# Group norm and layer norm ahead of a selective scan: GpSimd adds the two channel tiles of batches 1 to 3 before TensorE takes means and variances

## The chip, the cores and the metric

The kernel runs on one core of a Trainium2 chip. The core has five engines with a queue each: TensorE (PE in the profile, with its weight loads as PEld), VectorE (DVE), ScalarE (ACT), GpSimd (POOL) and SyncE (SP, which here only issues DMAs). They run side by side and wait for each other by semaphores. The metric is the device time of one execution in microseconds (us), as a median of several runs; lower is better. All data are fp32 unless a line says bf16.

## The reference, cut to what matters

The network has two layers on an input `x` of 4 batches x 256 channels x 1024 tokens. Layer 0 is a block with a group norm, a layer norm, four Mamba scans, attention and convolutions; layer 1 is attention and a mixture of experts. The change touches the first two norms of layer 0 alone:

```
def _gn(v, G=32, eps=1e-5):
    B_, C_, H_, W_ = v.shape
    g = v.reshape(B_, G, C_ // G, H_, W_)
    m = jnp.mean(g, axis=(2, 3, 4), keepdims=True)
    s = jnp.var(g, axis=(2, 3, 4), keepdims=True)
    return ((g - m) / jnp.sqrt(s + eps)).reshape(v.shape)

def layernorm(x, w, b, eps=1e-05):
    mu = x.mean(-1, keepdims=True)
    var = ((x - mu) ** 2).mean(-1, keepdims=True)
    return (x - mu) * jax.lax.rsqrt(var + eps) * w + b

x = x + _L0_conv_ref(_gn(x), ...)      # and inside it:
    xs = x.reshape(B, Cc, N).transpose(0, 2, 1)
    xn = layernorm(xs, norm_w, norm_b)          # over the 256 channels of each token
    xc = xn.reshape(B, N, NB, DM).transpose(2, 0, 1, 3)
    xm = mamba_v(xc, ...) + skip_scale * xc     # four independent selective scans
```

The layer norm needs, for each token, the mean and the variance over all 256 channels.

## The kernel before, in words

**Layout.** A batch is held as two channel tiles (`CT` = 2) of 128 partitions x 1024 tokens, `x[0]` and `x[1]`, and handled in halves of 512 tokens (`HALVES`). A sum over channels is a sum over partitions and over the two tiles, so it is done on TensorE.

**The norms of one batch, `normalise(b)` (L559 on).** Group norm: DVE sums of each tile (L568), a small matmul that adds them up by group (L569), squares with a running sum on ACT (L574), a second small matmul (L577), a copy (L580) and the inverse root by `small_root` (L548 to L557, a Newton iteration of twelve small DVE operations), then scale and shift in place (L586). Layer norm: for each half, TensorE multiplies a 128x128 matrix `avg` with 1/256 in each place by `x[0]` and then `x[1]`, accumulated in one PSUM bank, which leaves the mean of each token in all partitions (L592 to L595). DVE subtracts it from both tiles (L598). ACT writes the squares of both tiles to `sq` (L603), which is the place in `XM[b]` that the normalised batch will fill at last. The variance (L610 to L616) is taken the other way round: each block of 128 tokens of `sq` is the stationary operand and one column of `avg` the moving one, for both tiles, which leaves one column per block: 16 matmuls of one column. DVE copies them (L619) and runs `small_root` on 128x8. The result is put on the diagonal of `r` (L629: DVE for batch 0, POOL for the others), replicated to all partitions by a matmul with ones (L638), copied back to `r` by ACT (L652), and POOL multiplies both tiles by it (L654, 128x1024 each); ACT applies weight and bias (L656). For batch 0 a part of this is done by DVE and ACT straight from PSUM (L644, L648).

**The first front, `first_front` (L699 on).** For batch 0's first scan: a causal convolution as matmuls on 64 rows (L714, eight records for each half), SiLU (L717), two small projections (L720 and L750), a softplus (L722 to L731, in which DVE's L726 and L727 and POOL's L728 follow each other half by half), a DMA of `ds` (L732), a split of an fp32 tensor into three bf16 parts (L735 to L739), and the gathering of these parts into `U` by DMAs that SP and POOL issue (L744).

**The planner.** These two are not issued as written. Each operation is put in a plan with an engine, an estimated cost in ns, and what it reads and writes (`add(engine, cost, function, reads, writes, ...)`); `pre.run()` (L830) then sorts them by these estimates. Batch 0 and the first front are the plan's main line; `normalise(1)` to `normalise(3)` are added under `pre.beside(-1, -1, low=True)` (L821), which lets them fill gaps. So the order on every engine's queue follows the estimates. Results that stay in PSUM take one of a few banks (`pre.bank()`).

**Batch 3.** Its variances and the root are not part of the plan but of the list `behind`, (0, var) and (1, root): the first scan steps issue them, and later steps the diagonal (step 3), the replication (step 6) and the multiplication (from step 13).

**The scan loop (L832 on).** 256 steps in a written order; the scan is along the tokens, one step for each block of state rows. Step t: DVE multiplies the selected rows by B (L837), runs the scan over 1024 tokens (L840), POOL multiplies by C (L841); PE selects the rows of step t+2 (`select`, L778, from `U`), adds up the outputs of step t-2 (L789), SP fetches step t+4 (`fetch`, L766), ACT prepares step t+3 (`decay`, L771, an Exp of `dA` in place). Steps 0 and 1 are selected, and steps 0 to 2 decayed, by the plan. The next batch's front (L403 to L432) is mixed in by steps. `dBu`, which select fills, has two PSUM buffers, which the plan's banks share at first; in the trace the select of step 1 waits for scan 0.

After the loop come the rest of layer 0, layer 1's attention and the experts, which the change doesn't touch.

Of the kernel before, what the change touches and what calls it, by code (L numbers as in the profile page):

```python
# [13 lines left out]
ALU = mybir.AluOpType  # L14
# [6 lines left out]
P = 128  # L21
CT = C // P
# [136 lines left out]
class Plan:  # L159
# [32 lines left out]
    def add(self, engine, ns, emit, reads=(), writes=(), bank=None, take=False, give=False, pos=None, lag=0):  # L192
        reads, writes = list(reads), list(writes)
        banks = bank if isinstance(bank, list) else [] if bank is None else [bank]
        for bank in banks:
            (reads if give or engine != "PE" else writes).extend(bank.keys)
        deps = []
        for k in reads:
            if k in self.writer:
                deps.append(self.writer[k])  # L200
        for k in writes:
            deps.extend(self.readers.get(k, ()))
            if k in self.writer:
                deps.append(self.writer[k])
        op = dict(
            engine=engine, ns=ns, emit=emit, deps=deps, banks=banks, take=take, give=give, pos=pos, lag=lag,
            end=None, at=None, n=self.count,
        )
        self.count += 1
        for bank in banks:  # L210
            bank.ops.append(op)
        for k in reads:
            self.readers.setdefault(k, []).append(op)
        for k in writes:
            self.writer[k], self.readers[k] = op, []
        if self.group is None:
            self.main.setdefault(engine, []).append(op)
        else:
            self.group.append(op)
            self.side.setdefault(engine, []).append(op)  # L220
        return op
# [95 lines left out]
def body(tc, g, out):  # L317
    nc = tc.nc
    act, mm = nc.scalar.activation, nc.tensor.matmul
    ts, tt, stt = nc.vector.tensor_scalar, nc.vector.tensor_tensor, nc.vector.scalar_tensor_tensor  # L320
    HALVES = (slice(0, 512), slice(512, 1024))
# [4 lines left out]
    with pool("const", 1) as cp, pool("dram", 1, space=bass.MemoryType.DRAM) as drp, contextlib.ExitStack() as late:  # L326
# [7 lines left out]
        ident, grp, avg = cst[:, 0:P], cst[:, P : 2 * P], cst[:, 2 * P : 3 * P]  # L334
# [38 lines left out]
        with pool("mconst", 1) as mc, pool("front", 1) as fp, pool("dts", 2, space=bass.MemoryType.DRAM) as dsp, pool(  # L373
# [123 lines left out]
            with pool("scan", 6) as sp, pool("yps", 1, space=PSUM) as yps, pool("dps", 2, space=PSUM) as dps, pool("lnA", 1) as wp:  # L497
# [44 lines left out]
                def XS(b, ks=range(CT), hs=range(2)):  # L542
                    return [("xs", b, k, h) for k in ks for h in hs]

                def XN(b, ks=range(CT), hs=range(2)):
                    return [("xn", b, k, h) for k in ks for h in hs]
# [12 lines left out]
                def normalise(b):  # L559

                    x, r = xs[b], roots[b]

                    sq = dst = XM[b][:, :, XL : XL + N]
                    cols = slice(b * CT, (b + 1) * CT)
                    mine = [("gn", b)]
                    for k in range(CT):
                        j = b * CT + k
# [3 lines left out]
                    for k in range(CT):  # L571
                        j = b * CT + k
# [10 lines left out]
                    for k in range(CT):  # L583
                        j = b * CT + k
# [4 lines left out]
                    for h in range(2):  # L589
                        bank = pre.bank()  # L590

                        def mean(h=h, bank=bank):  # L592
                            for k in range(CT):
                                mm(bank.t, avg, x[k][:, HALVES[h]], start=k == 0, stop=k == CT - 1)
                        add("PE", 1720, mean, XS(b, hs=[h]), (), bank, take=True)  # L595
                        for k in range(CT):
                            add(
                                "DVE", 690, lambda k=k, h=h, bank=bank: tt(x[k][:, HALVES[h]], x[k][:, HALVES[h]], bank.t, ALU.subtract),  # L598
                                XS(b, [k], [h]), XS(b, [k], [h]), bank, give=k == CT - 1,
                            )  # L600
# [6 lines left out]
                    last = b == B - 1  # L607
                    bank = pre.bank()

                    def var():  # L610
                        for j in range(NT):
                            for k in range(CT):
                                mm(
                                    third[:, 520 + j : 521 + j] if last else bank.t[:, j : j + 1],
                                    sq[:, k, j * P : (j + 1) * P], avg[:, 0:1], start=k == 0, stop=k == CT - 1,
                                )  # L616

                    def root():
# [3 lines left out]
                    if last:  # L622
                        behind.extend([(0, var), (1, root)])
                        return
                    add("PE", 3500, var, XN(b), (), bank, take=True)
                    add("DVE", 2100, root, (), [("small", b)], bank, give=True)

                    def diagonal():
# [181 lines left out]
                with pre.beside(-1, -1):  # L810
                    weights()
                normalise(0)
                first_front()
                for t in range(4):
# [6 lines left out]
                with pre.beside(-1, -1, low=True):  # L821
                    for b in range(1, B):
                        normalise(b)
                    for i, step in fronts[1]:
                        if i < 0:
                            add("PE" if i < -1 else "ACT", 1720 if i < -1 else 1150, step, XN(0, [0]) + ["m_cu"], ["mm"])
# [4 lines left out]
                with tc.manual_schedule():  # L831
                    for t in range(NBLK + 9):  # L832
                        n, j = t // NJ, t % NJ
                        if t < NBLK:
# [4 lines left out]
                            hs = hss[t] = sp.tile([P, N], F32, tag="hs", name="hs")  # L839
# [35 lines left out]
        with pool("sets", 1) as wp, pool("work", 1) as kp, pool("ps2", 1, space=PSUM) as ps:  # L875
# [44 lines left out]
            add = plan.add  # L920
# [923 lines left out]
            for i in range(B * NT + 2):  # L1844
                b, unit = i // NT, (i - 2) // HT
# [25 lines left out]
        with pool("fin", 3) as fp, pool("rows", 1) as yp, pool("pfin", 4, space=PSUM) as pf:  # L1871
# [5 lines left out]
            for u in range(2 * B):  # L1877
                b, half = u // 2, u % 2
# [20 lines left out]
```

## Time and profile before

| | |
|---|---|
| runs | 3181.12, 3185.66, 3192.16 us (median 3185.66) |
| profiled execution | 3180.55 us, of which the profile's span is 3178.8 us |
| granted TensorE clock, mean of the span | 0.941 |
| busy over the span | PE 88%, DVE 64%, ACT 48%, POOL 39% |
| norms and first front | 0 to about 101 us |
| scan loop | about 101 to 1080 us |

How the profile is read: each instruction of one execution has a start and a duration, on its engine and with its line in the kernel. A row of a timeline has the start in us from the span's start, the duration, engine, line, operation, the output and input by the program's names, shape and type, and how many instructions were merged. Brackets say how long the engine sat idle before, and what released it. An f32 matmul shows as two records, so `x8` is four matmuls. PEclk is the clock that was granted to TensorE, 1.00 being full speed; it takes the values 0.5 and 1, and stretches show their mean. "q" after an engine's name is its instruction queue.

### The profile page before, as it was taken

The numbers are of one execution on the slowest core, as the hardware profiler recorded it, in microseconds if no ns is written. First come the engines' busy times: TensorE is split into PE (matmuls) and PEld (weight loads), VectorE is DVE, ScalarE is ACT, GpSimd is POOL, SyncE is SP. The second block draws the span as 40 slices with busy tenths as digits, with TensorE's granted clock in tenths as the row PEclk, the third lists the DMA queues.
The fourth block names the chain that finished last, engine by engine and source line by source line (L and its number), as shares of the span: only waits on it lengthen the run. The fifth ranks groups of instructions, "written<-read, shape, count | busy, mean of one in ns | idle before, by whom it ended". The sixth has DMA issues, their size and how long they took to land. (4 is left out here: it accounts for less than half of the span.)

```text
span 3178.8 us, 38805 instructions
## 1 busy us (share of the span) xinstructions
PE 2802.7 (88%) x15292; PEld 1592.1 (50%) x15292; DVE 2050.0 (64%) x2336; ACT 1533.2 (48%) x2102; POOL 1251.8 (39%) x790
## 2 busy tenths in 40 slices
PE   6788888888898689998899889988979998799996
PEld 3322222222222135555546455555536666699996
DVE  5799999999999656564866585486264545411112
ACT  3666566566655316455845764666343332211111
POOL 0687877777777500000100010001132334666662
PEclk7899999999989879999999989999989999899998
DMA  3576776676667400000000000000000002455445
GB/s 131 146 175 159 183 176 164 171 186 165 167 173 177 152 0 1 1 1 28 1 1 1 27 1 1 14 1 1 14 0 14 7 14 75 124 145 165 90 125 163
DMA packets 92874, 265.53 MB, mean 84 GB/s; under 512 B 18182, under 2 KB 36086, under 8 KB 89360
## 3 DMA queue, kind: packets, MB, share of 16 engines
q1 hardware_dynamic: 64000, 198.46, 23.6%
q0 software_dynamic: 26512, 60.35, 7.4%
q10 hardware_dynamic: 2176, 4.19, 0.3%
q8 instruction: 123, 2.02, 0.3%
q14 instruction: 63, 0.52, 0.1%
HBM read 291.70 MB, written 42.80 MB: 105 GB/s over the span
## 5 line engine op out<-in xcount | busy, mean ns | idle before, releaser
L841 POOL TENSOR_TENSOR hs<-hs,bc 128x1024 f32<-128x1024 f32 x256 | 603.2, 2357 | 246.4 <-DVE hs L840 236.1
L840 DVE TENSOR_TENSOR_SCAN hs<-dA,dBu 128x1024 f32<-128x1024 f32 x256 | 585.3, 2286 | 30.8 <-DVE dBu L837 1.9
L1106 DVE TENSOR_REDUCE nm<-s 128x1 f32<-128x1024 f32 x256 | 301.5, 1219 | 194.9 <-PE s L1101 193.9
L1111 ACT ACTIVATE pr<-s,nm 128x1024 f32<-128x1024 f32 x256 | 284.9, 1115 | 188.4 <-DVE nm L1106 185.7
L771 ACT ACTIVATE dA<-dA,aneg 128x1024 f32<-128x1024 f32 x256 | 289.1, 1145 | 164.7 <-DMA dA<-ds 155.1
L1125 PE MATMUL k<-const,pr 128*128 128x128 f32 x2048 | 296.4, 288 | 76.9 <-ACT pr L1111 51.1
L1125 PEld LDWEIGHTS k<-const,pr 128*128 128x128 f32 x2048 | 230.2, 145 | 186.1 <-ACT pr L1111 75.2
L837 DVE TENSOR_TENSOR dBu<-dBu,bc 128x1024 f32<-128x1024 f32 x256 | 309.9, 1211 | 18.3 <-PE dBu L778 18.1
L1175 POOL TENSOR_TENSOR b<-b 128x1024 f32<-128x1024 f32 (+1 forms) x15 | 30.3, 2019 | 684.6 <-ACT b L1171 665.3
L1101 PE MATMUL s<-b,b 32*128 32x512 f32 x1024 | 290.4, 654 | 5.1 <-ACT pr L1111 5.1
L778 PE MATMUL dBu<-U,pick 96*128 96x512 bf16 x512 | 161.9, 399 | 126.6 <-DVE hs L840 126.5
L1131 ACT COPY pT<-k 128x512 f32<-128x512 f32 x320 | 174.6, 592 | 171.0 <-PE k L1125 169.8
L789 PE MATMUL pY<-hs,const 128*128 128x512 f32 x512 | 243.1, 597 | 9.6 <-DVE u L481 9.6
L1774 PE MATMUL s<-pT,b 128*128 128x128 f32 x1920 | 236.0, 280 | 7.4 <-DMA b<-we,intse 6.2
L1774 PEld LDWEIGHTS s<-pT,b 128*128 128x128 f32 x1920 | 231.4, 196 | 13.2 <-issue 6.8
L778 PEld LDWEIGHTS <-pick 96*128 96x128 bf16 x512 | 34.6, 98 | 328.0 <-DVE hs L840 213.8
L1778 DVE TENSOR_TENSOR pT<-pT,s 128x512 f32<-128x512 f32 x72 | 49.3, 685 | 229.8 <-ACT pT L1777 229.6
L1131 DVE COPY pT<-k 128x512 f32<-128x512 f32 x192 | 131.4, 686 | 78.8 <-PE k L1125 74.7
L1145 PE MATMUL k<-pT,b 128*32 128x128 f32 x4096 | 150.0, 287 | 6.2 <-ACT pT L1131 4.0
L1101 PEld LDWEIGHTS s<-b,b 32*128 32x128 f32 x1024 | 104.3, 191 | 94.5 <-issue 76.5
L1145 PEld LDWEIGHTS k<-pT,b 128*32 128x32 f32 x4096 | 111.7, 114 | 69.9 <-issue 37.9
L789 PEld LDWEIGHTS pY<-hs,const 128*128 128x128 f32 x512 | 96.4, 191 | 98.1 <-issue 81.9
(445 smaller groups left out, 4647.6 us busy)
## 6 DMA issues: line engine op xcount, KB each, us to landing
dA<-ds SPq DMA_DIRECT2D x256, 512.0 KB, 4.7
dq<-parts SPq DMA_DIRECT2D x15, 768.0 KB, 4.2
U<-dq SPq DMA_DIRECT2D x45, 256.0 KB, 6.1
ds<-dt SPq DMA_DIRECT2D x16, 512.0 KB, 2.9
b<-x SPq DMA_DIRECT2D x4, 1024.0 KB, 7.1
acc<-pr SPq DMA_DIRECT2D x8, 512.0 KB, 7.6
xm<-x SPq DMA_DIRECT2D x4, 1024.0 KB, 5.0
tokens<-pr SPq DMA_DIRECT2D x8, 512.0 KB, 2.9
```

What stands on the lines that cost most here:

```text
L771: act(dAs[t], dAs[t], AF.Exp, scale=aneg[:, c : c + 1])
L789: mm(r["pY"][:, h], strip[:, P - DB - j * DB : 2 * P - DB - j * DB], hs[:, h], start=p == 0, stop=p == NJ - 1)
L837: tt(dBu, dBu, r["B"], ALU.mult)
L840: nc.vector.tensor_tensor_scan(hs, dAs.pop(t), dBu, 0.0, ALU.mult, ALU.add)
L841: nc.gpsimd.tensor_tensor(hs, hs, r["C"], ALU.mult)
L1101: mm(S[i][:, HALVES[h]], qT[rr, qt * P : (qt + 1) * P], kT[rr, HALVES[h]], start=True, stop=True)
L1106: "DVE", 1220, lambda i=i, u=u: nc.vector.tensor_reduce(nms[u], S[i], AX.X, ALU.max, negate=True),
L1111: "ACT", 1330, lambda i=i, u=u, hd=hd: act(prs[u % 4], S[i], AF.Exp, bias=nms[u], scale=1.0, accum_out=rss[b % 2][:, k, qt, hd : hd + 1]), ...
L1125: nc.tensor.transpose(bank.t[:, j * P : (j + 1) * P], prs[u][:, c0 : c0 + P], ident)
L1131: lambda dst=dst, bank=bank, on_act=on_act: (nc.scalar.copy if on_act else nc.vector.tensor_copy)(dst, bank.t),
L1145: mm(bank.t[i * HD : (i + 1) * HD, 0:P], v[:, 4 * jh + j, hd * HD : (hd + 1) * HD], pTs[m][jh][:, i, j * P : (j + 1) * P], start=j == 0, s ...
L1774: mm(p12[:, a, c], wbufs[w][:, o : o + P], xT[:, k], start=k == 0, stop=k == CT - 1)
```

## The change

For batches 1 to 3 POOL adds the two tiles of a half into `sq[:, 0]` before the mean, so that one matmul per half is left of two; and after ACT's squares POOL adds `sq[:, 1]` to `sq[:, 0]`, half by half, so that eight one-column matmuls are left of sixteen. `sq[:, 0]` is used twice, first for the sums and then for the squares. Batch 0 stays as it is. The estimates in the plan change with it: each addition 1180 on POOL, the mean 860 instead of 1720, the variance 1800 instead of 3500. For batch 3 the additions before the variance are part of the plan, and the variance itself stays in `behind`. XS(b, ks, hs) names the keys of x's tiles and halves, XN(b, ks, hs) those of `sq`.

```
@@ in normalise(b), for h in range(2) @@
+                        if b:
+
+                            add(
+                                "POOL", 1180, lambda h=h: nc.gpsimd.tensor_tensor(sq[:, 0, HALVES[h]], x[0][:, HALVES[h]], x[1][:, HALVES[h]], ALU.add),
+                                XS(b, hs=[h]), XN(b, [0], [h]),
+                            )
+
                         def mean(h=h, bank=bank):
+                            if b:
+                                mm(bank.t, avg, sq[:, 0, HALVES[h]], start=True, stop=True)
+                                return
                             for k in range(CT):
                                 mm(bank.t, avg, x[k][:, HALVES[h]], start=k == 0, stop=k == CT - 1)
-                        add("PE", 1720, mean, XS(b, hs=[h]), (), bank, take=True)
+                        add("PE", 860 if b else 1720, mean, XN(b, [0], [h]) if b else XS(b, hs=[h]), (), bank, take=True)
@@ behind the squares @@
+                    if b:
+                        for h in range(2):
+                            add(
+                                "POOL", 1180, lambda h=h: nc.gpsimd.tensor_tensor(sq[:, 0, HALVES[h]], sq[:, 0, HALVES[h]], sq[:, 1, HALVES[h]], ALU.add),
+                                XN(b, hs=[h]), XN(b, [0], [h]),
+                            )
+
                     def var():
                         for j in range(NT):
-                            for k in range(CT):
+                            for k in range(1 if b else CT):
                                 mm(
                                     third[:, 520 + j : 521 + j] if last else bank.t[:, j : j + 1],
-                                    sq[:, k, j * P : (j + 1) * P], avg[:, 0:1], start=k == 0, stop=k == CT - 1,
+                                    sq[:, k, j * P : (j + 1) * P], avg[:, 0:1], start=k == 0, stop=b > 0 or k == CT - 1,
                                 )
@@
-                    add("PE", 3500, var, XN(b), (), bank, take=True)
+                    add("PE", 1800 if b else 3500, var, XN(b), (), bank, take=True)
```

## The prediction

> **What bounds the kernel now.** The whole-span page comes first: VectorE is busy 64% of 3178.8 us, TensorE 88%, GpSimd 39%. These are averages over stages; the change touches only the first. Its chain of waits covers the last 52 us (DMAs, `out`) and says nothing of it. So I read the busy time by stretches: DVE is the third pair, POOL the fifth, then the granted TensorE clock.
>
> ```profile
> core 0: us, PE busy (x) PEld busy (x) DVE busy (x) ACT busy (x) POOL busy (x), PEclk, DMA share, GB/s
> ...
> 101.00:120.00 19.00, 10.56 (x46) 6.12 (x46) 11.26 (x19) 12.45 (x13) 9.30 (x4) 0.70 0.46 114
> 120.00:200.00 80.00, 64.49 (x169) 22.26 (x170) 77.73 (x48) 52.85 (x48) 68.16 (x30) 0.94 0.67 166
> 200.00:1080.00 880.00, 757.75 (x1994) 237.82 (x1995) 836.09 (x504) 528.89 (x475) 661.22 (x286) 0.95 0.67 170
> ```
>
> From 120 to 1080 us DVE is full: 77.73 of 80 (97%) and 836.09 of 880 (95%), one scan step after another. From 101 to 120 it is busy for 11.26 of 19. Nothing in the scan loop's DVE work changes after its first steps, so what the change does to the kernel is **how far it moves the start of the third scan**. The timeline of DVE, in the columns start, duration, engine, line, shows what that scan waits for.
>
> ```profile
> 96.84 2.48 DVE L598 TENSOR_TENSOR xs<-xs,dBu 128x512 f32<-128x512 f32 x4 [2.52 <-PE dBu L594]
> 101.00 1.23 DVE L837 TENSOR_TENSOR dBu<-dBu,bc 128x1024 f32<-128x1024 f32 x1 [1.69 <-PE dBu L778]
> 102.34 2.29 DVE L840 TENSOR_TENSOR_SCAN hs<-dA,dBu 128x1024 f32<-128x1024 f32 x1
> 105.76 1.23 DVE L837 TENSOR_TENSOR dBu<-dBu,bc 128x1024 f32<-128x1024 f32 x1 [1.13 <-PE dBu L778]
> 107.09 2.29 DVE L840 TENSOR_TENSOR_SCAN hs<-dA,dBu 128x1024 f32<-128x1024 f32 x1
> 115.33 0.17 DVE L619 COPY smalls<-pY 128x8 f32<-128x8 f32 x1 [5.95 <-PE pY L613]
> 115.53 0.92 DVE L550 TENSOR_SCALAR smalls<-smalls 128x8 f32<-128x8 f32 x1
> ...
> 118.59 1.23 DVE L837 TENSOR_TENSOR dBu<-dBu,bc 128x1024 f32<-128x1024 f32 x1
> 119.85 2.29 DVE L840 TENSOR_TENSOR_SCAN hs<-dA,dBu 128x1024 f32<-128x1024 f32 x1
> ```
>
> Scans start at 102.34, 107.09 and 119.85. Between the second and the third DVE idles 5.95 us for batch 3's variances (L613), then computes their root (L619, twelve small operations of L550 to L557). The timeline of PE has the other side:
>
> ```profile
> 87.93 3.63 PE L613 MATMUL pY<-const,xm 128*128 128x1 f32 x32
> 91.42 5.38 PE L594 MATMUL dBu<-xs,const 128*128 128x512 f32 x8
> 96.73 3.70 PE L403 MATMUL mm<-xm,m_cu 64*128 64x512 f32 x8
> 100.36 0.61 PE L778 MATMUL dBu<-U,pick 96*128 96x512 bf16 x2
> 104.69 1.03 PE L778 MATMUL dBu<-U,pick 96*128 96x512 bf16 x2 [3.72 <-DVE hs L840]
> 105.51 1.91 PE L638 MATMUL pY<-r,const 128*128 128x512 f32 x2
> ...
> 111.60 3.63 PE L613 MATMUL pY<-const,xm 128*128 128x1 f32 x32
> ```
>
> An f32 matmul is two records here. Step 0's select (L778, 100.36) stands behind batch 2's variances, batch 3's means and eight L403 records; its U had landed at 98.0 (PE's queue waits for it from 91.4 to 98.0) and its decay ran at 96.15. Step 1's select waits for scan 0, whose PSUM it reuses.
>
> **What it removes.** Six 512-column matmuls (half of L594 for three batches; batch 3's eight records took 5.38, so 2.7 each) and 24 one-column ones (half of L613: 3.96, 3.63 and 3.63 us, so 5.6). That is some 13 us of PE. Of it little lies on the path: DVE's 5.95 us before scan 2 is the one long wait for an L613, and half of that is 1.8 us.
>
> **What it adds.** Twelve POOL additions of 128x512. The nearest row is L728, the same shape with both inputs in SBUF:
>
> ```profile
> 58.05 1.89 POOL L629 TENSOR_TENSOR dA<-const,smalls 128x1024 f32<-128x1024 f32 x1 [2.58 <-DVE gst L580]
> ...
> 82.51 1.28 POOL L728 TENSOR_TENSOR dt<-dt,e 128x512 f32<-128x512 f32 x1
> ...
> 111.77 4.64 POOL L654 TENSOR_TENSOR xm<-hs,r 128x1024 f32<-128x1024 f32 x2
> ```
>
> 12 x 1.28 = 15.4 us of POOL, which before 101 us is mostly idle. Batch 1's four and batch 2's mean pair are covered. Not covered are the pair in front of batch 3's variances and a new order.
>
> **What it moves.** New costs change the planner's order; the two programs' instruction lists show it. Batch 2's variances, its root, batch 3's means and subtractions, all ahead of step 0 before, now come behind the first scans. PE: select 0, select 1, batch 2's variances, batch 3's means, select 2, L414, batch 2's replicate (L638), batch 3's variances, select 3. DVE: mul 0, scan 0, mul 1, copy of batch 2's variances, scan 1, twelve small ones, four subtractions (L598), copy and twelve small ones of batch 3, mul 2, scan 2. Batch 3's group root and batch 2's subtractions move up between the two halves of `first_front` (between L727 and L726). SP issues step 1's dA before the last U parts.
>
> **The sum, term by term.**
>
> 1. *Up to scan 0: -1 (from -2.4 to +4).* Gain: select 0 no longer waits for 5.38 + 3.63 of PE, but cannot pass U: 100.36 - 98.0 = 2.4 at most. L714 may start about 2 us sooner, since batch 1's variances in front (50.95 to 54.9) halve. Loss: dA's transfers land 2.32 apart (100.36, 102.68), and one more of them is now ahead of U. On DVE, L727 of half 0 ends at 78.84; 2.5 of root and 2.48 of subtractions follow, so L726 and L727 of half 1 end at about 85.2, POOL's L728 at 86.5, and L731 starts 0.8 after the present 85.72; up to 4 more if that root is held (term 4). I take -1: clean gains and losses nearly cancel.
> 2. *Scan 0 to scan 1: +2 (from +0.7 to +2.3).* The copy between mul 1 and scan 1 waits for 16 one-column records behind select 1. Batch 3's 32 took 3.63 (clock up), batch 0's 6.21 (clock down, 32.78 to 38.99): so 1.8 or 3.1, plus 0.1 and a copy of 0.17, against a mul of 1.23 that runs beside. PE has been nearly idle since select 0; in the stretch from 115 to 120, as idle, its clock was 0.55. I take 3.1.
> 3. *Scan 1 to scan 2, without holds: +3.5 (from +2.5 to +4.5).* From scan 1's end to scan 2's start is 119.85 - 109.38 = 10.47 now. After: root of batch 2 2.5 (91.80 to 94.3 in this trace), diagonal on POOL 1.89, replicate 3.5 (105.51 to 108.98), variances 1.8 to 3.1, copy and root 2.5, mul 2 1.26: 13.5 to 14.8. A second chain beside it, subtractions to 5.0, L419 and four squares on ACT to 6.2, POOL's second addition to 7.6, ends before the replicate (8.0) and so adds nothing; were the diagonal early it would be next.
> 4. *Held small operations: +3.5 (from 0 to +7).* L550 by its own rows, minimum, median and maximum:
>
> ```profile
> L550 DVE TENSOR_SCALAR gst<-gst x4: 168/169/1893, 21.8 to 63.8; 128x2 f32<-128x2 f32 x4
> L550 DVE TENSOR_SCALAR smalls<-smalls x4: 171/202/916, 39.2 to 115.5; 128x8 f32<-128x8 f32 x4
> ```
>
> The long ones are the two beside a POOL operation: the 1893 ns beside L629 from 58.05 to 59.94, ending with it, and the 916 ns at 115.53, ending with L654 (111.77 + 4.64 = 116.41). Subtractions and scans, with an operand in PSUM, ran beside POOL at their usual length. After the change the root of batch 2 starts exactly when POOL multiplies scan 1's result (2.35): +2. Batch 3's root falls beside batch 2's two L654 (4.64) and may be held up to twice where once cost 0.75: +1.5.
>
> Sum: -1 + 2 + 3.5 + 3.5 = **+8**. The profiled execution took 3180.55 (span 3178.8), so 3188.6 of its own; the median of the runs shown is 5.1 higher, 3185.66, so 3193.7.
>
> The Trainium skill, "GPSIMD Engine Reference", section 1 (Specifications), says that GpSimd's SBUF interfaces are shared with VectorE, with contention for a DVE instruction in a two-port mode or with two SBUF inputs. It speaks against this change: each of the twelve additions could hold a VectorE operation. By it term 4 stays and more could be added in the first half; without any such sharing the sum would be +4.5. The rows of L550 agree with it, and L598, unstretched with one operand in PSUM, does too.
>
> **Rivals.**
>
> - *Not slower: the clock rises in the front (-1; from -10 to +3; chance 0.22).* L714's two groups ran 55.27 to 62.46 and 63.24 to 70.43, all at 0.50, 14.4 us for sixteen records. Now its eight matmuls stand in a row, closer to batch 1's means. If one step of the clock (it changes at 50.8, 54.2 and 74.66, multiples of 3.41 us) catches full speed there, 3.4 us of half speed is worth 1.7; two such and no held operation give -3.4 + 4.5 - 2 = -1, which is 3184.7. It decides from the point where PE has 3.41 dense us just before L714. Against it: the 64-row L714 itself stayed at 0.50 throughout, and half 1 still waits for half 0's SiLU.
> - *The front is held (+15; from +13 to +20; chance 0.18).* Batch 3's group root, now between the halves of `first_front`, falls beside L728 and two L654 (78.98 to 83.73 plus 2.43). Held across them it loses 3 to 4, everything to U and select 0 slips, and +8 becomes +12 to +15: about 3200.
> - *It saves PE work that nobody waits for, and the order costs nothing (0 to +4; chance 0.1).* DVE idles 1.69, 1.13 and 5.95 in the loop's head; the moved work could fill these. For it: the subtractions leave the stretch before 101. Against: the chain in term 3 is serial through four engines. About 3187.
>
> **How the numbers follow.** The forecast, +4 to +13, has 0.5. About 0.3% (9.6 us) is what a measurement of this kernel can tell from no change. Slower by more: the front held (0.18) and the upper part of the forecast, 0.21: 0.39. Faster by more: the far end of the first rival, 0.04. Within: 0.57. For the range I leave out the first rival's lower half and the held front's upper end: -1.7 to +17.3, so 3184 to 3203.
>
> **What would show it.** Scan 0 near 101; 6.8 instead of 4.75 from scan 0 to scan 1, with the copy of batch 2's variances in between; 18 to 20 instead of 12.76 from scan 1 to scan 2; a first root operation of about 2.2 us ending with POOL's L841; then 3.53 per step as now. It is wrong if scan 2 starts before 121 (no hold, or the chain overlaps), if the front's clock is 1.00 from 55 to 70, or if steps after scan 2 are longer than 3.53.

## The result, and the profile after

| | before | changed |
|---|---|---|
| runs (5 each, us) | 3179.65 to 3192.16, median 3185.66 | 3196.82 to 3207.74, median 3201.49 |
| ratio | 1 | 1.0052, 95% interval 1.0041 to 1.0064 |
| span of the profiled execution | 3178.8 us | 3199.7 us |
| granted TensorE clock | 0.941 | 0.934 |

The change costs 15.8 us. The forecast was +8, half of it: the direction and the wide range of 3184 to 3203 hold, the forecast's own span of +4 to +13 does not. The busy time by stretches (DVE the third pair) shows the gap where the forecast looked for it: from 120 to 200 DVE is now busy for 72.66 instead of 77.73 us, since the loop fills up later, and from 92 to 101 PE does nothing, where before it was busy all the time. The first row is the kernel before, the others the changed one.

```profile
92.00:101.00 9.00, 8.97 (x18) 3.24 (x16) 4.42 (x16) 5.87 (x8) 2.90 (x4) 0.83 1.03 227
...
92.00:101.00 9.00, 0.00 (x0) 0.00 (x0) 1.33 (x3) 7.02 (x8) 6.64 (x9) 0.54 0.90 214
101.00:120.00 19.00, 11.95 (x30) 6.51 (x30) 13.16 (x21) 6.02 (x8) 6.58 (x3) 0.59 0.55 133
120.00:200.00 80.00, 62.83 (x170) 23.53 (x171) 72.66 (x55) 51.20 (x50) 64.16 (x30) 0.87 0.54 141
200.00:1080.00 880.00, 760.02 (x1980) 239.48 (x1979) 832.00 (x502) 528.70 (x475) 660.89 (x287) 0.94 0.66 171
```

The next view is the timeline of DVE in the changed kernel (start, duration, engine, line; idle time before it and its releaser in brackets). L743 and L744 are the former L726 and L727, L748 the former L731, L636 the former L619, L608 the former L598, L752 the former L735, L854 and L857 the former L837 and L840.

```profile
72.53 0.69 DVE L743 TENSOR_SCALAR dBu<-e 128x512 f32<-128x512 f32 x1 [11.68 <-ACT e L742]
73.26 0.69 DVE L744 SCALAR_TENSOR_TENSOR e<-dBu,e 128x512 f32<-128x512 f32 x1
73.87 0.15 DVE L580 COPY gst<-pY 128x2 f32<-128x2 f32 x1
74.05 0.17 DVE L550 TENSOR_SCALAR gst<-gst 128x2 f32<-128x2 f32 x1
74.26 1.14 DVE L551 CAST gst<-gst 128x2 f32<-128x2 int32 x1
75.43 2.27 DVE L552 TENSOR_SCALAR gst<-gst 128x2 int32<-128x2 f32 x1
77.73 2.26 DVE L555 SCALAR_TENSOR_TENSOR gst<-gst 128x2 f32<-128x2 f32 x1
...
81.47 2.47 DVE L608 TENSOR_TENSOR hs<-hs,dBu 128x512 f32<-128x512 f32 x4
83.86 0.69 DVE L743 TENSOR_SCALAR pY<-e 128x512 f32<-128x512 f32 x1
...
85.91 1.33 DVE L752 TENSOR_TENSOR e<-dt,u 128x512 f32<-128x512 f32 x1
87.16 1.76 DVE L586 TENSOR_SCALAR xs<-xs,gst 128x1024 f32<-128x1024 f32 x1
88.84 0.68 DVE L748 TENSOR_TENSOR dt<-dt,pY 128x512 f32<-128x512 f32 x1
...
104.59 2.29 DVE L857 TENSOR_TENSOR_SCAN hs<-dA,dBu 128x1024 f32<-128x1024 f32 x1
108.01 1.23 DVE L854 TENSOR_TENSOR dBu<-dBu,bc 128x1024 f32<-128x1024 f32 x1 [1.13 <-PE dBu L795]
111.22 0.17 DVE L636 COPY smalls<-pY 128x8 f32<-128x8 f32 x1 [1.97 <-PE pY L630]
111.30 2.28 DVE L857 TENSOR_TENSOR_SCAN hs<-dA,dBu 128x1024 f32<-128x1024 f32 x1
...
113.68 2.35 DVE L551 CAST smalls<-smalls 128x8 f32<-128x8 int32 x1
...
117.96 2.47 DVE L608 TENSOR_TENSOR xs<-xs,dBu 128x512 f32<-128x512 f32 x4
125.46 0.17 DVE L636 COPY smalls<-pY 128x8 f32<-128x8 f32 x1 [5.03 <-PE pY L630]
125.66 1.16 DVE L550 TENSOR_SCALAR smalls<-smalls 128x8 f32<-128x8 f32 x1
126.85 2.27 DVE L551 CAST smalls<-smalls 128x8 f32<-128x8 int32 x1
...
132.31 2.29 DVE L857 TENSOR_TENSOR_SCAN hs<-dA,dBu 128x1024 f32<-128x1024 f32 x1
```

The kernel before has these rows for the same front; between L727 of half 0 and L726 of half 1 DVE only waits, for 1.23 us:

```profile
77.42 0.69 DVE L726 TENSOR_SCALAR dBu<-e 128x512 f32<-128x512 f32 x1 [9.64 <-ACT e L725]
...
80.07 0.69 DVE L726 TENSOR_SCALAR pY<-e 128x512 f32<-128x512 f32 x1 [1.23 <-ACT e L725]
...
85.72 0.68 DVE L731 TENSOR_TENSOR dt<-dt,pY 128x512 f32<-128x512 f32 x1
```

The rows of L550, on which the forecast's hold was built, show only a part of the holds (minimum, median, maximum in ns): which of a root's operations is caught depends on when POOL starts, and in the front and the loop it is mostly L551 and those behind it.

```profile
L550 DVE TENSOR_SCALAR gst<-gst x4: 169/170/1894, 21.6 to 74.1; 128x2 f32<-128x2 f32 x4
L550 DVE TENSOR_SCALAR smalls<-smalls x4: 145/665/1626, 36.2 to 125.7; 128x8 f32<-128x8 f32 x4
```

Two roots that stood ahead of the loop or in idle time now stand in the chain. Batch 3's group root (73.87 to 81.5) separates the two halves of the first front, and half 1's L743 waits behind it and the subtractions until 83.86. Batch 2's root comes behind scan 1. The third scan starts at 132.31 instead of 119.85, and then the distance stays: 12.37 us at scan 3, and still at scan 24. The timeline of PE shows the other side: it is idle for 13.24 us, waiting for U, while the work that used to fill this time comes behind the selects.

```profile
86.98 1.98 PE L403 MATMUL mm<-xm,m_cu 64*128 64x512 f32 x4
102.21 1.01 PE L795 MATMUL dBu<-U,pick 96*128 96x512 bf16 x2 [13.24 <-DMA U<-parts]
106.94 1.04 PE L795 MATMUL dBu<-U,pick 96*128 96x512 bf16 x2 [3.72 <-DVE hs L857]
107.76 3.41 PE L630 MATMUL pY<-const,xm 128*128 128x1 f32 x16
111.04 3.76 PE L601 MATMUL dBu<-xm,const 128*128 128x512 f32 x4
```

The timeline of POOL says why the root's operations are long: each held one ends with a POOL operation. L745 ends at 75.36 and L551 at 75.40; the two L671 end at about 77.65 and 79.97, and L552 and L555 at 77.70 and 79.99.

```profile
74.09 1.27 POOL L745 TENSOR_TENSOR dt<-dt,e 128x512 f32<-128x512 f32 x1 [10.68 <-ACT dA L669]
75.32 4.65 POOL L671 TENSOR_TENSOR xm<-hs,dA 128x1024 f32<-128x1024 f32 x2
85.42 1.27 POOL L745 TENSOR_TENSOR dt<-dt,e 128x512 f32<-128x512 f32 x1 [5.45 <-DVE e L744]
86.64 1.72 POOL L623 TENSOR_TENSOR xm<-xm 128x512 f32<-128x512 f32 x1
...
95.80 1.28 POOL L623 TENSOR_TENSOR xm<-xm 128x512 f32<-128x512 f32 x1
```

**A measure that doesn't depend on one execution.** The two spans differ by 20.9 us, the medians by 15.8. To see what is fixed and what is scatter, both kernels were profiled again (before_again, change_again below). The start of the first front's convolution (L714, later L731) moves by 5.2 us between two executions of the kernel before (55.27 and 50.11) and by 3.1 between two of the changed one (51.20 and 54.34), with different clocks ahead of it. Three stretches after the front's first half, each from start to start, repeat better, within 1.7 us. They are the base of all that follows: (A) from half 0's L726/L743 to scan 0, (B) from scan 0 to scan 1, (C) from scan 1 to scan 2.

| kernel | A | B | C | sum against before | time against before (ratio, interval) |
|---|---|---|---|---|---|
| before, two profiles | 24.92, 26.58 | 4.75, 4.75 | 12.76, 12.76 | 0 | 1 |
| the change, two profiles | 32.06, 32.47 | 6.70, 6.70 | 21.01, 19.42 | +15.9 | 1.0052 (1.0041 to 1.0064), 1.0046 (1.0029 to 1.0062) |
| mean_only | 27.40 | 4.75 | 12.77 | +1.7 | 1.0007 (0.9997 to 1.0018) |
| var_only | 30.67 | 6.70 | 20.02 | +14.1 | 1.0038 (1.0024 to 1.0052) |
| root_later | 27.39 | 6.71 | 20.23 | +11.1 | 1.0029 (1.0017 to 1.0040) |
| roots_psum | 29.49 | 6.78 | 18.70 | +11.7 | 1.0050 (1.0037 to 1.0064) |
| oldvar | 27.51 | 4.75 | 12.55 | +1.6 | 1.0003 (0.9990 to 1.0015) |
| oldvar1 | 27.60 | 4.75 | 12.56 | +1.7 | 0.9997 (0.9983 to 1.0011) |
| m_var3 | 26.92 | 4.75 | 12.53 | +0.9 | 1.0001 (0.9988 to 1.0014) |
| var1 | 30.72 | 4.75 | 13.71 | +5.9 | 1.0015 (1.0001 to 1.0028) |

The sum is A + B + C less the mean of the two profiles of before (43.26). For the kernels of this table it lies within the interval of the measured time (1 us is 0.0003); roots_psum lies at the lower edge of its own.

### The profile page after: what moved, and what is told of

Read it like the earlier page. It is cut to its first block, busy times and chain, and to the rows that moved or that the text cites. A ratio compares the mean times of both kernels' runs of the same rounds, so it can differ in the third digit from the quotient of the medians.

```text
span 3199.7 us, 38694 instructions
## 1 busy us (share of the span) xinstructions
PE 2806.2 (88%) x15232; PEld 1585.6 (50%) x15232; DVE 2063.3 (64%) x2336; ACT 1532.6 (48%) x2101; POOL 1269.1 (40%) x802
## 5 line engine op out<-in xcount | busy, mean ns | idle before, releaser
L857 DVE TENSOR_TENSOR_SCAN hs<-dA,dBu 128x1024 f32<-128x1024 f32 x256 | 585.4, 2287 | 30.7 <-DVE dBu L854 1.5
L854 DVE TENSOR_TENSOR dBu<-dBu,bc 128x1024 f32<-128x1024 f32 x256 | 310.1, 1211 | 29.4 <-PE dBu L795 29.4
```

The costliest lines, as they stand in the source:

```text
L854: tt(dBu, dBu, r["B"], ALU.mult)
L857: nc.vector.tensor_tensor_scan(hs, dAs.pop(t), dBu, 0.0, ALU.mult, ALU.add)
```

## The experiments

The theory after the result: the loss is the order that the change's new estimates make (theory A), with small operations held by POOL on top; rival B: the additions themselves cost, by their work or by the extra hop between engines. Each kernel is the changed one with the edit shown, unless it says otherwise.

**mean_only** keeps the additions before the means and takes the variances as before (the edit is at the additions behind the squares, at `var` and at its estimate):

```
-                    if b:
+                    if b in ():
-                            for k in range(1 if b else CT):
+                            for k in range(1 if b in () else CT):
-                    add("PE", 1800 if b else 3500, var, ...)
+                    add("PE", 1800 if b in () else 3500, var, ...)
```

> Only the additions in front of the means (6 of the 12), the variances as before; batch 2's variances and root and all of batch 3's subtractions stand ahead of step 0 again. Theory A (the loss is the order behind the additions in front of the variances, plus small VectorE operations held by GpSimd): scan 2 starts 0 to 4 us sooner than before, the time is 0 to 5 us under before. Theory B (the additions themselves cost, by their work on GpSimd or their extra hop between engines): half of the change's loss, +6 to +10.

Measured 3195.3 against 3191.53 us for before on the same chip. Six additions cost no time that can be told from none (at most 5.7 us by the interval), against theory B's 6 to 10. But nothing is gained either: theory A's 0 to 5 us did not come. Batch 3's subtractions move up into the front in this order, and A is 27.40.

**var_only** is the opposite, the same edit made at the additions before the mean, at `mean` and at its estimate.

> Only the additions in front of the variances, the means as before. Theory A: batch 2's variances again come behind select 1 and its root behind scan 1, so scan 2 starts 8 to 13 us later than before and the time is +8 to +16. Theory B: half of the loss, +6 to +10.

Measured 3203.8 against 3191.53. The interval is 7.7 to 16.6 us, so the time alone leaves room for theory B too. The stretches speak for theory A: B and C are as in the change, with batch 2's root behind scan 1. The variance's half carries nearly the whole loss.

**root_later** keeps batch 3's group root out of the first front by one more thing to wait for:

```
-                    add("DVE", 2100, scale, mine, mine)
+                    add("DVE", 2100, scale, mine + ([("dt", 1)] if b == B - 1 else []), mine)
```

> The change, but batch 3's group root may start only when half 1's dt of the first front is done, so it no longer stands between the halves of that front. Theory A: the hold of 5.2 us there is gone, half 1's L743 comes 4 us sooner and scan 0 3 to 4 us sooner than in the change (at about 101); the loop's head (18 to 21 from scan 1 to scan 2) stays, so 3 to 4 us under the change. Theory C (the front isn't what sets scan 0, the transfers are): scan 0 stays at 104.6 and the time stays.

Measured 3201.54 against 3191.53: a third of the loss or more is gone. A falls by 4.9 to 27.39, C stays at 20.23. Theory A holds, theory C of this run doesn't.

**roots_psum** keeps the change's order and lets each small operation of the roots read or write PSUM:

```
-                    ts(v, v, EPS, None, ALU.add)
-                    nc.vector.tensor_copy(r, v.bitcast(mybir.dt.int32))
-                    ts(tmp.bitcast(mybir.dt.int32), r, -0.5, float(0x5F3759DF), ALU.mult, ALU.add)
+                    w, q, p, s = (third[:, at + i * n : at + (i + 1) * n] for i in range(4))
+                    ts(v, var, EPS, None, ALU.add)
+                    ts(w, var, EPS, None, ALU.add)
+                    nc.vector.tensor_copy(q, w.bitcast(mybir.dt.int32))
+                    ts(p.bitcast(mybir.dt.int32), q, -0.5, float(0x5F3759DF), ALU.mult, ALU.add)
+                    nc.vector.tensor_copy(r, p)
                     for i in range(3):
-                        a, c = (tmp, r) if i % 2 == 0 else (r, tmp)
-                        stt(c, a, -0.5, a, ALU.mult, ALU.mult)
-                        stt(c, v, 1.0, c, ALU.mult, ALU.mult)
-                        stt(c, c, 1.5, a, ALU.add, ALU.mult)
+                        stt(s, p, -0.5, r, ALU.mult, ALU.mult)
+                        stt(s, s, 1.0, v, ALU.mult, ALU.mult)
+                        stt(r if i == 2 else p, s, 1.5, r, ALU.add, ALU.mult)
+                        if i < 2:
+                            nc.vector.tensor_copy(r, p)
```

> The change with the same order on every engine, but each small operation of the roots reads or writes PSUM (same formula; two more operations in a group root, three more in a token root, about 0.4 and 0.6 us). Theory A: none of them is longer than 0.3 us, the front's h1 comes about 4.5 us sooner, the stretch from scan 1 to scan 2 falls from 21.0 to about 17, and the time is 6 to 9 us under the change. Theory D (the long small operations wait for something else, such as a semaphore or the order): they stay long whatever memory they read, and the time is 1 to 2 us over the change.

The hold is what it was said to be, and its price is not. The rows of two lines whose counterparts (L551 and L555) were held, with minimum, median and maximum in ns:

```profile
L553 DVE CAST pY<-pY x8: 155/168/175, 21.7 to 127.4; 128x2 f32<-128x2 int32 x4, 128x8 f32<-128x8 int32 x4
```

```profile
L557 DVE SCALAR_TENSOR_TENSOR pY<-pY,gst x12: 168/168/168, 22.3 to 80.2; 128x2 f32<-128x2 f32 x12
L557 DVE SCALAR_TENSOR_TENSOR pY<-pY,smalls x12: 174/174/174, 39.3 to 129.7; 128x8 f32<-128x8 f32 x12
```

No operation is longer than 0.18 us, in the same places beside the same POOL operations, so theory D falls. Yet the time was 3207.17 against 3191.53, no better than the change. Its DVE timeline says where the gain went:

```profile
80.64 0.16 DVE L559 SCALAR_TENSOR_TENSOR gst<-pY,gst 128x2 f32<-128x2 f32 x1
82.77 2.48 DVE L611 TENSOR_TENSOR hs<-hs,dBu 128x512 f32<-128x512 f32 x4 [1.97 <-PE dBu L604]
...
127.10 0.17 DVE L551 TENSOR_SCALAR smalls<-pY 128x8 f32<-128x8 f32 x1 [6.97 <-PE pY L633]
```

The subtractions now wait 1.97 us for batch 2's means, and batch 3's root waits 6.97 for its variances, where it waited 5.03. By the stretches 4.2 us were saved, after an estimated 1.8 for the nine added operations in them (0.2 each). By the time nothing was saved; the interval reaches from 11.8 to 20.4 us over before, and the stretches give +11.7. Six more added operations, in batch 0's two roots, stand ahead of half 0's L743, where the stretches don't reach: an estimated 1.2 us. Whether anything else took the gain stays open.

**oldvar** is the sharpest test: all twelve additions, all the matmuls saved, one number of the plan put back.

```
-                    add("PE", 1800 if b else 3500, var, XN(b), (), bank, take=True)
+                    add("PE", 3500, var, XN(b), (), bank, take=True)
```

> The change with all twelve additions and all the matmuls it saves; only one number is put back, the plan's estimate for the variance (3500 instead of 1800). That restores the order of before: batch 2's variances and root and batch 3's subtractions stand ahead of step 0. Theory A (the loss is the order that the new estimate makes): scan 0 to scan 1 is 4.75 again, scan 1 to scan 2 about 10.5 to 12 (batch 3's variances take half of 3.6), scan 2 starts 0 to 5 us before that of the kernel before, the time is 0 to 5 us under before and 12 to 20 under the change. Theory B (the additions or their extra hop cost): the time stays 8 or more over before.

Measured 3185.89 against 3183.0. The loss is gone with all the additions in place, and with it rival B, which put it at 8 or more. The gain didn't come. The DVE timeline shows a reason in C:

```profile
105.33 2.29 DVE L857 TENSOR_TENSOR_SCAN hs<-dA,dBu 128x1024 f32<-128x1024 f32 x1
111.78 0.17 DVE L636 COPY smalls<-pY 128x8 f32<-128x8 f32 x1 [4.17 <-PE pY L630]
111.98 0.40 DVE L550 TENSOR_SCALAR smalls<-smalls 128x8 f32<-128x8 f32 x1
112.42 2.27 DVE L551 CAST smalls<-smalls 128x8 f32<-128x8 int32 x1
...
117.88 2.29 DVE L857 TENSOR_TENSOR_SCAN hs<-dA,dBu 128x1024 f32<-128x1024 f32 x1
```

Batch 3's variances do come 1.8 us sooner (a wait of 4.17 for one of 5.95), and its root, that much earlier, is then held through both of POOL's multiplications instead of the end of the second.

A holds the other reason, of about the same size: 27.51 against 24.92 and 26.58 before. The order is not quite that of before. Batch 3's subtractions stand in the front, and its last L748 starts 11.79 us after half 0's L743 instead of 8.30; so they do in mean_only (12.27) and m_var3 (11.78). The rows of DVE, and below them the one of POOL:

```profile
84.86 0.68 DVE L748 TENSOR_TENSOR dt<-dt,pY 128x512 f32<-128x512 f32 x1
85.45 2.37 DVE L752 TENSOR_TENSOR e<-dt,u 128x512 f32<-128x512 f32 x2
88.40 2.78 DVE L754 TENSOR_TENSOR e<-e,parts 128x512 f32<-128x512 f32 x2 [0.57 <-ACT parts L753]
...
85.86 4.78 POOL L623 TENSOR_TENSOR xm<-xm 128x512 f32<-128x512 f32 x3 [2.04 <-ACT xm L613]
```

The additions are not free either: beside three of them L752 and L754 take 5.15 us instead of 2.67. Most of that is hidden, for mean_only has no such hold there and the same A (27.40). The interval leaves at most 4.8 us for all of it.

**m_var3** has the additions before all means but before batch 3's variances alone (`b in (3,)` in place of `b in ()` in mean_only's edit).

> The additions in front of all means and in front of batch 3's variances alone (eight of twelve); batch 1 and 2 take their variances by 16 matmuls. Theory A: the order of before, scan 1 to scan 2 about 10.5 to 12, the time 0 to 5 us under before. Theory B: two thirds of the change's loss, +8.

Measured 3183.75 against 3183.0, with the same hold in C. Theory A's order of the loop's head is there, its gain isn't.

**before_again** and **change_again** are the two kernels unchanged.

> The kernel before, unchanged, for a second profile. If the scan loop from scan 2 to the last scan takes 961.5 us again, the 965 to 967 of the change and of the experiments are an effect of theirs; if it takes 963 or more, the difference after scan 2 is scatter from one execution to the next. The time is that of before, within 3 us.

> The change, unchanged, for a second profile: scan 2 starts 11 to 14 us after that of the kernel before, with the same long operations in the roots (about 2.3 us beside GpSimd's multiplications); the time is +10 to +17. If the loop's steps after scan 2 agree with the first profile's to 0.5 us in sum, what they lose is fixed; if not, it is scatter.

Measured 3187.46 and 3198.72 against 3183.0. From scan 2 to the last scan the kernel before took 961.48 us in its first profile and 964.84 in the second, the change 966.57 and 965.11. So the 5 us that the first pair of profiles showed after scan 2 are mostly scatter; a mean difference of 2.7 is left, and 8 kernels of this study with the same loop lie between 962.4 and 967.0.

**var1** is the kernel with additions for batch 1's variances alone, two of twelve (`b in (1,)` at the variance, none at the means).

> Only batch 1's variances get the additions (two of twelve) and the estimate of 1800; everything else as before. Batch 3's group root again stands in the first front, batch 2's variances stay ahead of step 0, half of batch 3's subtractions come behind scan 1. Theory A (order): the stretch from half 0's L743 to the last dt of the front takes 12 to 16 us instead of 8.29, scan 0 to scan 1 stays 4.75, the time is +3 to +10. Theory B (each addition costs): two of twelve, +2 to +3, with that stretch at 8 to 9.

Measured 3190.04 against 3185.72, and the front's stretch took 13.85 instead of 8.29: theory A's number. The time (0.3 to 8.9 us over before) alone fits both theories. One batch's additions with their estimate are enough to put batch 3's root in the front.

**oldvar1** puts the estimate back for batch 1 only: `1800 if b > 1 else 3500`.

> The change with the estimate of 3500 for batch 1's variances alone (1800 for batches 2 and 3). On every engine the order is that of the kernel in which all three estimates were put back. So the same time as that: within 3 us of before, 12 to 18 under the change; scan 0 to scan 1 4.75, scan 1 to scan 2 12.5. If batch 2's or batch 3's estimate or work mattered beside the order, it would lie above.

Measured 3183.36 against 3185.72: as before, with the stretches of oldvar. With all else as in the change, batch 1's estimate alone decides whether the loss is there. Whether batch 2's alone would do the same was not run, nor was it followed why the planner turns at this number.

**oldvar_late** and **before_late** try to gain what the change was near: the 5.95 us that DVE waits for batch 3's variances. ScalarE copies them out of PSUM in step 1, and the root moves to step 4:

```
-                        behind.extend([(0, var), (1, root)])
+                        def read():
+                            nc.scalar.copy(small[:, 0], third[:, 520 : 520 + NT])
+
+                        def late_root():
+                            small_root(small[:, 1], small[:, 0], small[:, 2])
+
+                        behind.extend([(0, var), (1, read), (4, late_root)])
-                behind += [(3, diagonal), (6, replicate), ...
+                behind += [(5, diagonal), (8, replicate), ...
```

> The change in the order of before (estimate 3500), and batch 3's variances are copied from PSUM by ScalarE in step 1, with the root on VectorE in step 4 in place of step 1 and the diagonal and replication two steps later. If VectorE's wait for these variances ahead of scan 2 is what is left to gain in this stretch, scan 1 to scan 2 falls from 12.5 to 3.5 to 6, one root of 2.5 to 5 is added later, and the time is 3 to 7 us under before. If the select of step 2 or the decay of step 2 is late next, it falls by 2 or less.

> The kernel before with the same late root for batch 3, without any of the additions. As with them: scan 1 to scan 2 falls from 12.76 to 3.5 to 6 and the time is 3 to 7 us under before. If halving the variances on TensorE is worth anything on the path here, this lies up to 2 us above the one with the additions; if not, the two are the same.

Measured 3193.49 and 3190.66 against 3185.72. Both forecasts missed: the first is slower (1.0022, 1.0007 to 1.0037), the second can't be told from before (1.0013, 0.9998 to 1.0028). C falls as forecast, to 4.33 and 4.32, 8.2 us less than in oldvar and 8.4 less than before. The following steps give all of it back: from scan 2 to the last scan they take 976.77 and 977.06 us, where before took 961.48 and 964.84 and oldvar 966.97. The waits of before_late between 95 and 125 us name the takers (waiting engine and line, waited-for, total, times, longest):

```profile
PE pY L795 <- ACT smalls L624: 6.7, 1, 6.7
...
DVE e L425 <- ACT mm L422: 3.4, 1, 3.4
```

PE's first sum of outputs needs the PSUM tile that ACT reads late, behind L422, and DVE's L425 waits for the same queue. By these rows the long wait ahead of scan 2 covered work of ACT that is due anyway.

No kernel of the study is faster than before beyond its interval.

## Why the prediction was right or wrong, point by point

- *The third scan's start carries the change*: right. A + B + C gives +15.9 and the medians +15.8.
- *The range*: it held because it reached into the rival "the front is held". The sum's own +4 to +13 did not hold.
- *The additions are covered and the TensorE work saved is worth little*: right within what the time can tell; oldvar has both and takes the time of before. They are not free: see L752 and L754 there.
- *Term 2, scan 0 to scan 1, +2*: measured 1.95. The variances took 3.41 us for 16 records at a clock of 0.50; batch 3's 16, at 1.00, took 1.84 (start 123.51).
- *Terms 3 and 4, scan 1 to scan 2, +7 together*: measured 8.25 and 6.66. The sum was right, the split wasn't. Without holds (roots_psum) the stretch is 18.70, of which some 1.2 are the six added operations at 0.2 each: 4.7 over before instead of 3.5. That leaves 2.7 of the mean of 20.2 for the holds instead of 3.5, because batch 3's variances are late next.
- *Term 1, up to scan 0, -1*: **the step that failed**, "clean gains and losses nearly cancel". From half 0's L743 on, stretch A grew by 6.5. That is beyond the term's own range of -2.4 to +4. The gains weren't there: no sooner start of L714 can be seen (52.7 before, 52.8 after, as means of two profiles that differ by 3 to 5), and select 0 could not use the freed PE because U itself was late. The losses were mis-sized: the root between the halves took 7.6 us with its holds instead of 2.5, and a held L752 and a held L586 came ahead of the last L748, which the text had not counted. The front's stretch from L743 to the last dt went from 8.29 to 16.31, where +0.8 was expected.
- *The rival "the front is held", 0.18, about 3200*: it named the place and the end that was measured. Its mechanism was half of it: without holds of the roots A falls by 2.8 (roots_psum), without the root at that place by 4.9 (root_later). The profile had given no reason to hold the roots in the loop and not the one in the front; POOL's L728 and L654 stood beside it in the page of before.
- *The rival of the clock*: no. From 55 to 75 us the clock was 0.66 and 0.58 in the two profiles of the changed kernel, 0.51 and 0.69 in those of the kernel before.
- *The rival that the order costs nothing*: no. In oldvar and oldvar1 it is the order that the loss goes away with.
- *After scan 2, 3.53 per step as now*: right, as a median step (3.54 in both kernels). The distance didn't change from scan 3 to scan 24, and what comes later is mostly scatter.

The Trainium skill's sentence on contention ("GPSIMD Engine Reference", section 1, Specifications) agrees with roots_psum: it names VectorE instructions in a two-port mode or with two SBUF inputs, and the root's operations with a PSUM operand never took more than 0.18 us, where without one they took up to 2.35.

## What to carry to other kernels

Where a planner sorts work by estimates, a change of estimate is part of the change: compare the instruction lists, and try the new work with the old number before blaming the work. A removed stall is worth only the distance to the next one, so ask of each stretch what is late next; here holds of 10.4 us in sum (5.2 in the front, 2.2 and 3.1 in the loop) were worth 4.2 in the stretches, net of the operations added, and taking away a wait of 5.95 us made the kernel no faster. Compare stretches between two marks on the same engine and take two profiles of each kernel: the start of one stage moved by 5 us between executions of the same kernel.

## What the runs showed of the hardware that was not expected

- A held small VectorE operation lasts until the POOL operation beside it ends, and the next small one can be caught by the next POOL operation: three in a row took 1.14, 2.27 and 2.26 us where 0.17 is usual. A larger one ends later: L752 (0.68 us when alone) took 1.33 and ended 0.55 us after POOL's L745.
- POOL's operations get longer too: the addition at 86.64 took 1.72 us, and 1.28 at 95.80 with VectorE idle. Beside it ran the end of VectorE's L752 (until 87.24) and an L586 (1.76 instead of 0.80); which of the two lengthened it is not shown.
